# A graph attention kernel: second-layer softmax whose sums come out of the last product

## The chip, the cores and the metric

The kernel runs on one core of one Trainium2 chip. The metric is the device time of one execution in microseconds (us). Before the change it is 2752.51 us, the median of three runs (2750.7, 2752.51 and 2756.27).

The core's engines work in parallel, each through its own instruction stream: TensorE (PE in the profile; PEld is its loading of weights) multiplies matrices into eight PSUM banks, VectorE (DVE) and ScalarE (ACT) compute element by element and empty the banks, GpSimd (POOL) issues some of the transfers and does small work, SyncE (SP) issues the other transfers. An instruction waits until those whose results it needs are done; a stream is worked off in order.

## The reference

32 independent graphs (B = 32) have N = 512 nodes with D = 512 features each. After a layer normalisation and a ReLU come two graph attention layers, the first with 4 heads of 256 features, the second with one head of 512; the input is added at the end.

```python
h = jnp.maximum(_layernorm(x, axis=-1), 0.0)
# gat_layer(h, mask, W, a_src, a_dst, bias):
xl = (x @ W).reshape(B, N, H, F)
asrc = einsum('bnhf,hf->bnh', xl, a_src); adst = einsum('bnhf,hf->bnh', xl, a_dst)
e = leaky_relu(asrc[:, :, None, :] + adst[:, None, :, :], 0.2)
e = where(mask[..., None], e, -1e9)
attn = softmax(e, axis=1)                 # over the sources s
out = einsum('bsdh,bshf->bdhf', attn, xl) # concat (layer 1) or mean (layer 2), + bias
# layer 1, then elu, then layer 2; x + result
```

The mask is the adjacency matrix with the diagonal added. All is fp32.

## The kernel before

**Batches and stages.** A batch is one graph. Node rows are cut into NT = 4 blocks of P = 128 partitions. The main loop (`for i in range(B - 1)`) overlaps batches: while one batch is in its second layer, the next is in its first. A turn of the loop has these products on TensorE: the rest of layer 1's attention product (`gather1`), layer 1's projection of a later batch (`project1`), the second layer's attention product (`gather2`), and the second layer's projection of the next batch (`project2`). The last batch, 31, has plain versions of some of these.

**Products.** Most matrix products are split into 2 x 2 blocks and done in seven block products instead of eight (the Winograd form of Strassen's scheme), numbered 1 to 7. `sevens` (L1170) issues them for `project2` and `gather2`. The result of a product is accumulated in PSUM on top of earlier ones; `ACC` (L1154) says in which bank of its unit: products 1, 6, 7 and 4 follow each other in bank "a", 5 and 3 in "b", 2 has bank "g". A unit u (0 or 1) is a block of 128 output rows within each half. After each product `put` moves what stands in the bank (an eviction): product 1's result is a part of block (0, 0), product 2's is the other part, 6 and 3 belong to block (0, 1), 4 to (1, 0), 5 and 7 to (1, 1) (`BLOCK`, L1152). In `gather2` every one of the 14 evictions of a batch is a VectorE addition of 128x256 from the bank onto the residual tile, which holds the input x and is stored when its block row is complete. The next product into the same bank waits for the eviction. `NEAR` (L1580) is the order of the products: 1, 5, 6, 2, 7, 3, 4, each for both units. `PARTS` (L1213) is the order for batch 29, whose product is interleaved with the last projection. Each block product of `gather2` is two matmuls of 128x128 by 128x256.

The right-hand blocks of `gather2` are the second layer's features, in `xl2` (for the last two batches in memory that is free by then); `project2` leaves them in two halves of 257 columns, and the 257th column of a half is a score of the node. `scores_2` (L1527) reads these columns. `sums2` (L1554) forms the sums and differences of blocks that the products need: t1, t2, t4 in three free slots of the x tiles (`xs`, L604), others in place.

**Softmax.** It runs over sources, which lie on the partitions in the product, so it is done in two passes (`Soft`). `columns` makes the score columns and spreads one of them over all partitions (`spread`: a transposition on VectorE, a small transfer to DRAM, and one back that repeats it 128 times). `first` (L1005), with targets on the partitions, does four blocks d of 128 targets, each over all 512 sources:

```python
act(..., e, o[:, j, :], AF.Prelu, bias=z[:, 1, j, d : d + 1], alpha=SLOPE)    # leaky ReLU of the score sums
dve(..., nc.vector.tensor_tensor_reduce, out=e3, in0=e3, in1=mt[:, :, d, :], ...)  # mask, and -maximum
act(..., e, e, AF.Exp, bias=low[:, 0, d : d + 1], scale=-1.0, accum_out=low[:, 1, d : d + 1])  # sums
```

then a logarithm of the four sums, and spreads (score - maximum - log of the sum) over the partitions. `second` (L1058), with sources on the partitions, forms the scores again (VectorE multiply-adds), adds the mask by accumulating transfers from DRAM (issued by GpSimd), and takes the exponential (ScalarE), which is then the normalised attention matrix p.

**Order of the work.** Nothing is issued as the functions above run: `act`, `dve`, `dma`, `accumulate` and `pe` (L645 to L660) add a job to a `Program` with an estimated cost and the keys that it reads and writes. `Program.order` lays TensorE's jobs down in the order in which they were added, simulates all engines, and searches for an order of the other engines' jobs that lets TensorE wait least. A change of any job thus changes the order of the whole. `Banks.take` gives a bank; with `kept`, only a bank whose columns were last written up to that width, since a matmul is then to add to what another engine put there (a fork: ScalarE copies one bank into another, and a product is added on top).

The profile names the helper line where a job is recorded: L646 ScalarE, L649 VectorE, L652 SP's transfers, L657 the accumulating transfers, L663 matmuls. In the profile's tile names mm is a bank, p the attention matrix, t the residual, l the tile e of the first pass, rr and as the spread rows, z and low small columns, x the x slots.

Of the kernel before, what the change touches and what calls it, by code (L numbers as in the profile page):

```python
# [15 lines left out]
AF = mybir.ActivationFunctionType  # L16
OP = mybir.AluOpType
# [3 lines left out]
P = 128  # L21
EPS = 1e-5
SLOPE = 0.2
BIG = 2.0**100
# [488 lines left out]
def tile_gat(  # L513
# [46 lines left out]
    KQ = KT // 2  # L560
    KH = FT // 2
    W2H = DO // 2 + 1
    assert N == 512 and D == 512 and DO == D and FH == 256 and H == 4

    sbuf = ctx.enter_context(tc.tile_pool(name="sbuf", bufs=1))
# [35 lines left out]
    hs = sbuf.tile([P, 2, KH, N // 2], F32, name="hs")  # L601
    hs4 = sbuf.tile([P, KQ, N // 2], F32, name="hs4")

    xs = slots("x", NT, [P, D])  # L604
    adjs = slots("adj", 2, [P, N], I32)
    xrs = slots("xr", 3, [P, N])
    ls = slots("l", 3, [P, N])
# [5 lines left out]
    rrs = slots("rr", 2, [P, 2, N])  # L613
    das = slots("das", 2, [2 * NT, P], F32, dram)
    drs = slots("drr", 2, [2 * NT, P], F32, dram)
    mds = slots("dm", 3, [P, NT, N], BF16, dram)
    stats = slots("stats", 2, [P, NT, nc.vector.BN_STATS_DIM + nc.vector.BN_AGGR_DIM + 1])
    zs = slots("z", 4, [P, 5, 2, NT])
    lows = slots("low", 3, [P, 4, NT])
    banks = Banks(tiles("mm", 8, [P, 512], F32, psum))  # L620


# [4 lines left out]
                tensor=w1_sb.tensor, offset=w1_sb.offset + NT * (DO + 2) + i * NT * N,  # L627
                ap=[w1_sb.ap[0], [N, NT], [1, N]],
# [7 lines left out]
        ap=[w1_sb.ap[0], [1, NT * N // 2]],  # L636
# [6 lines left out]
    prog = Program()  # L643

    def act(cost, reads, writes, *a, **k):  # L645
        prog.add("ACT", cost, reads, writes, lambda: nc.scalar.activation(*a, **k))  # L646

    def dve(cost, reads, writes, f, *a, **k):
        prog.add("DVE", cost, reads, writes, lambda: f(*a, **k))  # L649
# [302 lines left out]
    class Soft:  # L952
# [52 lines left out]
        def first(self, h, parts=((0, NT),)):  # L1005


            i, j = divmod(h, self.g)
            zk, z, keys = self.z[i]
            ok, o = self.asr[i]  # L1010
            tk, mt = MASKT[self.b]
            wk, low = lows.take()
            zj = z[:, 1, j]
            self.rr[h] = []
            for d0, d1 in parts:
                for d in range(d0, d1):
# [33 lines left out]
                v = bass.AP(tensor=low.tensor, offset=to, ap=[low.ap[0], [1, 2 * n]])  # L1050
                self.rr[h].append((d0, d1, *self.spread(v, [wk + (2, d0)], 2, rrs, drs, n)))
            lows.give(wk)
            if j == self.g - 1:
                ass.give(ok)
            if self.layer == 2:
                mts.give(tk)

        def second(self, h):  # L1058
            i, j = divmod(h, self.g)
# [107 lines left out]

        return put

    def sevens(left, right, rkeys, put, kh, units, width, order, seeds={}):  # L1170


        bank, sixth = {}, len({u for u, _ in order})
        for u, n in order:
            m = units[u][0]
            acc, first = ACC[n], n in (1, 2, 5)
            if first:
                bank[u, acc] = banks.take(width, M if n in seeds else 0)
            bk, bt = bank[u, acc]
            ps = bt[:, :width]  # L1180
            if first and n in seeds:
                first = False
# [28 lines left out]
    FOUR = LAST + tuple((u + 2, n) for u, n in LAST)  # L1211

    PARTS = (  # L1213
        (0, 1), (1, 1), (0, 2), (1, 2), (0, 5), (1, 5), (0, 6), (1, 6), (0, 3), (1, 3), (0, 7), (1, 7),
        (0, 4), (1, 4),
    )

# [284 lines left out]
    def x2_key(b, t, c):  # L1502
        return ("x2", b, t, c) if b >= B - LATE else ("xl2", t, c)
# [50 lines left out]
    def sums2(b, soft, place=None, keys=None):  # L1554

        pk, p = soft.p[0]
        blocks = half_blocks(p, KQ, lambda r, c: p_keys(pk, (2 * c, 2 * c + 1), (r,)))
        left = sums(blocks, KQ, 0.59, KQ, place, keys)
        v = x2(b)
        b11, b12, b21, b22 = (  # L1560
            (
                v[:, 2 * r : 2 * r + 2, c * W2H : c * W2H + M],
                [x2_key(b, 2 * r + i, c) for i in range(2)],
            )
            for r in range(2) for c in range(2)
        )
        t1, t2, t4 = (
            (t.rearrange("p (k f) -> p k f", f=M), [k]) for k, t in (xs.take() for _ in range(3))
        )

        def op(to, a, c):
            dve(0.59, a[1] + c[1], to[1], nc.vector.tensor_sub, to[0], a[0], c[0])

        op(t1, b12, b11)
        op(t2, b22, t1)
        op(b12, b22, b12)
        op(t4, b21, t2)
        return left, {1: b11, 2: b21, 3: b22, 4: t4, 5: t1, 6: t2, 7: b12}

    NEAR = tuple((u, n) for n in (1, 5, 6, 2, 7, 3, 4) for u in range(2))  # L1580

    def gather2(b, soft, blocks, order=NEAR):
        left, right = blocks
        xr = XR.pop(b)
        upper = [2, 2]

        def put(n, u, bk, ps):
            r, c = BLOCK[n - 1]
            d = 2 * r + u[0]
            place, xk, xt = xr[d]  # L1590
            to = xt[:, c * M : (c + 1) * M]
            dve(ADD, [bk, xk + (c,)], [xk + (c,)], nc.vector.tensor_tensor, to, ps, to, op=OP.add)

            upper[u[0]] -= n in (2, 3)
            if n == 4 or r == 0 and upper[u[0]] == 0:
                upper[u[0]] = -1
                dma(0.65, [xk, xk + (0,), xk + (1,)], (), out[b, d * P : (d + 1) * P, :], xt)
                place.give(xk)

        yield from sevens(  # L1600
            left, lambda n, u, k: right[n][0][:, k, :], lambda n: right[n][1], put, KQ,
            [(0,), (1,)], M, order,
        )
        ps_.give(soft.p.pop(0)[0])
        for n in (4, 5, 6):
            xs.give(right[n][1][0])
# [194 lines left out]
```

## Time and profile before

| | |
|---|---|
| runs | 2750.7, 2752.51, 2756.27 us |
| the profiled execution's span | 2756.9 us, 4.4 us above the median |
| TensorE busy | 2732.9 us, 99% of the span |
| VectorE busy | 2595.0 us, 94% |
| ScalarE busy | 2281.9 us, 83% |
| GpSimd busy | 326.5 us, 12% |
| mean granted TensorE clock | 0.999 |

Busy time is the time in which at least one instruction of the engine was running; instructions of one engine overlap a little, so that the mean duration of one is longer than the distance from one to the next. Each fp32 matmul leaves two records. The span runs from the first to the last instruction of the program.

### The profile page before, as it was taken

What the parts mean: (1) busy time and instruction counts of PE and PEld (TensorE: products, weight loads), DVE (VectorE), ACT (ScalarE), POOL (GpSimd) and SP (SyncE); (2) the same over time, 40 slices, a digit from 0 to 9 for tenths busy, and PEclk for the clock granted to TensorE, in tenths of its full rate; (3) what the DMA queues carried; (4) which work ended last, traced back from release to release, by engine and by line L of the source; (5) the groups of instructions that cost most, each with busy time, mean ns of one, the idle gap of its engine ahead of it and who ended that gap; (6) DMA issues with size and microseconds to landing.
All of it is one profiled execution on the core that took longest, in us unless ns stands there. A gap on an engine that the chain in (4) does not pass through costs nothing.

```text
span 2756.9 us, 41901 instructions
## 1 busy us (share of the span) xinstructions
PE 2732.9 (99%) x12490; PEld 2367.0 (86%) x12490; DVE 2595.0 (94%) x6744; ACT 2281.9 (83%) x4871; POOL 326.5 (12%) x356
## 2 busy tenths in 40 slices
PE   7999999999999999999999999999999999999999
PEld 6688888888888888888888888888888888888887
DVE  8999999999999999999999999999999999999996
ACT  5978898888888888988889887888888898888973
POOL 0111110101111011111011110111111111101110
PEclk9999999999999999999999999999999999999999
DMA  8756866667676677666776666766666766777663
GB/s 225 182 162 181 206 177 173 182 182 194 174 193 176 177 184 206 179 168 183 187 207 173 182 176 183 191 188 182 178 182 180 213 173 172 185 183 199 169 169 108
DMA packets 375863, 502.10 MB, mean 182 GB/s; under 512 B 222804, under 2 KB 227668, under 8 KB 375636
## 3 DMA queue, kind: packets, MB, share of 16 engines
q1 hardware_dynamic: 329844, 332.68, 43.3%
q0 software_dynamic: 45792, 166.74, 24.7%
q8 instruction: 100, 1.64, 0.2%
q14 instruction: 127, 1.04, 0.1%
HBM read 316.41 MB, written 51.31 MB: 133 GB/s over the span
## 4 chain that ended last, share of the span: by engine, by line
PE 97%; DMA 1%; ACT 1%; DVE 0%; SPq 0%; issue 0%; ACTq 0%
PE mm L663 97%; DMA x<-adj 0%; DMA w_sb<-dm 0%; ACT l L646 0%; DMA w_sb<-in_L_gnn_W_dram 0%; DMA as<-das 0%; DMA das<-as 0%; SPq L652 0%; DVE h L649 0%; ACT x L646 0%; DVE hs L649 0%; ACT ht L646 0%; DVE w_sb L649 0%; ACT w_sb L646 0%; DVE xl L649 0%
## 5 line engine op out<-in xcount | busy, mean ns | idle before, releaser
L663 PE MATMUL mm<-w_sb,hs 128*128 128x257 f32 (+2 forms) x3032 | 696.4, 380 | 2.2 <-ACT xl L646 1.6
L663 PEld LDWEIGHTS mm<-w_sb,hs 128*128 128x128 f32 x3032 | 575.3, 190 | 87.7 <-ACT xl L646 2.4
L657 POOL DMA_DIRECT2D p<-dm x314 | 274.3, 878 | 2330.5 <-DVE p L649 1312.6
L646 ACT ACTIVATE l<-l,low 128x512 f32<-128x512 f32 x640 | 458.2, 719 | 23.1 <-DVE low L649 20.6
L663 PE MATMUL mm<-w_sb,h 128*128 128x257 f32 x2056 | 467.9, 379 | 0.0
L663 PE MATMUL mm<-p,xl 128*128 128x256 f32 (+1 forms) x1984 | 466.6, 383 | 0.0
L649 DVE SCALAR_TENSOR_TENSOR p<-rr,z 128x512 f32<-128x512 f32 (+1 forms) x636 | 453.8, 739 | 0.0
L646 ACT ACTIVATE l<-as,z 128x512 f32<-128x512 f32 x640 | 436.7, 714 | 17.4 <-DMA as<-das 16.7
L663 PEld LDWEIGHTS mm<-w_sb,h 128*128 128x128 f32 x2056 | 389.2, 189 | 58.1 <-issue 0.5
L646 ACT ACTIVATE p<-p,z 128x512 f32<-128x512 f32 (+1 forms) x636 | 422.0, 718 | 11.3 <-DVE p L649 8.4
L649 DVE CUSTOM_DVE_ANT_1 l<-l,mt 128x512 f32<-128x512 f32 x640 | 424.8, 681 | 4.4 <-ACT l L646 2.3
L663 PEld LDWEIGHTS mm<-p,xl 128*128 128x128 f32 x1984 | 377.3, 190 | 58.8 <-issue 6.9
L663 PE MATMUL mm<-w_sb,ht 128*128 128x258 f32 x1802 | 419.5, 382 | 2.9 <-ACT ht L646 2.9
L663 PEld LDWEIGHTS mm<-w_sb,ht 128*128 128x128 f32 x1802 | 340.7, 190 | 55.7 <-ACT ht L646 3.3
L646 ACT ACTIVATE h<-mm,b_sb 128x256 f32<-128x256 f32 (+1 forms) x504 | 226.2, 475 | 184.5 <-PE mm L663 183.8
L646 ACT ACTIVATE xl<-mm 128x258 f32<-128x258 f32 (+2 forms) x686 | 258.3, 380 | 84.0 <-PE mm L663 80.6
L649 DVE TENSOR_TENSOR xl<-xl,mm 128x258 f32<-128x258 f32 (+1 forms) x526 | 215.4, 416 | 51.6 <-PE mm L663 47.4
L663 PE MATMUL mm<-t,hs 128*128 128x256 f32 x992 | 226.1, 380 | 0.0
L663 PEld LDWEIGHTS mm<-t,hs 128*128 128x128 f32 x992 | 189.0, 191 | 26.1 <-DVE t L649 0.3
L649 DVE TENSOR_TENSOR t<-mm,t 128x256 f32<-128x256 f32 (+1 forms) x424 | 171.7, 417 | 15.8 <-PE mm L663 13.3
L646 ACT ACTIVATE xr<-h 128x512 f32<-128x512 f32 x256 | 157.6, 624 | 34.5 <-DVE h L649 32.9
L663 PE MATMUL mm<-xl,p 128*128 128x256 f32 (+1 forms) x752 | 179.3, 387 | 0.0
(132 smaller groups left out, 3451.2 us busy)
## 6 DMA issues: line engine op xcount, KB each, us to landing
p<-dm POOLq DMA_DIRECT2D x314, 512.0 KB, 4.9
rr<-drr SPq DMA_DIRECT2D x159, 512.0 KB
x<-in_x_dram SPq DMA_DIRECT2D x129, 256.0 KB
adj<-in_adj_dram SPq DMA_DIRECT2D x128, 256.0 KB
as<-das SPq DMA_DIRECT2D x64, 512.0 KB
t<-in_x_dram SPq DMA_DIRECT2D x124, 256.0 KB
out_dram<-t SPq DMA_DIRECT2D x124, 256.0 KB
dm<-m SPq DMA_DIRECT2D x64, 256.0 KB
```

The costliest lines, as they stand in the source:

```text
L646: prog.add("ACT", cost, reads, writes, lambda: nc.scalar.activation(*a, **k))
L649: prog.add("DVE", cost, reads, writes, lambda: f(*a, **k))
L657: lambda: nc.gpsimd.dma_start(to, at, accum_op=OP.add), size,
L663: f(*a, **k)
```

## The change

In the second layer of all batches but the last, the softmax is no longer normalised before the product.

- `first` calls the new `bounds` where `summed` says so (layer 2, not the last batch). It takes the masked maximum directly over the spread scores (the leaky ReLU is monotonic, so it can be applied to the four maxima afterwards, by two small VectorE operations). The Prelu, the Exp with its sums and the logarithm on ScalarE fall away. What is spread is (score - maximum).
- The sums come out of the product: the score column behind the blocks B11 and B21, and one behind t1, are set to 1.0 by GpSimd (two memsets in `sums2`), and the products 1, 2 and 5 take 257 columns instead of 256. The x slots are made two columns wider for this.
- Product 2 must stand on top of product 1 for the sums of the upper rows, so ScalarE copies the bank of product 1 into product 2's bank (a fork), and product 2 adds to it. Product 1 is then not evicted by itself.
- `put` takes the reciprocal of the 257th column after products 2 and 5 (VectorE, one column each), and each of the 12 evictions that are left multiplies by it and adds.
- The orders change so that 2 comes ahead of 6 in `NEAR`, and 5 ahead of 2 in `PARTS`.

```diff
     def first(...):
             for d0, d1 in parts:
+                if self.summed():
+                    self.bounds(j, d0, d1, wk, low, ok, o, keys, zk, zj, h)
+                    continue
...
+        def bounds(self, j, d0, d1, wk, low, ok, o, keys, zk, zj, h):
+            tk, mt = MASKT[self.b]
+            n = d1 - d0
+            for d in range(d0, d1):
+                lk, e = ls.take()
+                dve(
+                    0.62, [ok, tk + (0,), tk + (1,)], [lk, wk + (0, d)], nc.vector.tensor_tensor_reduce,
+                    out=e.rearrange("p (t r) -> p t r", r=P),
+                    in0=o[:, j].rearrange("p (t r) -> p t r", r=P), in1=mt[:, :, d, :], scale=-1.0,
+                    scalar=BIG, op0=OP.add, op1=OP.min, accum_out=low[:, 0, d : d + 1],
+                )
+                ls.give(lk)
+            dve(TINY, ..., nc.vector.tensor_sub, low[:, 1, d0:d1], zj[:, d0:d1], low[:, 0, d0:d1])
+            dve(TINY, ..., nc.vector.scalar_tensor_tensor,
+                low[:, 0, d0:d1], low[:, 1, d0:d1], SLOPE, low[:, 1, d0:d1], op0=OP.mult, op1=OP.max)
+            dve(TINY, ..., nc.vector.tensor_tensor, ..., op=OP.subtract)
+            self.rr[h].append((d0, d1, *self.spread(v, [wk + (2, d0)], 2, rrs, drs, n)))
...
     def sevens(..., forks=False):
             if first:
-                bank[u, acc] = banks.take(width, M if n in seeds else 0)
+                bank[u, acc] = banks.take(width, M if n in seeds else width if forks and n == 2 else 0)
...
+            if forks and n == 2:
+                first = False
+                ak, at = bank[u, "a"]
+                act(0.29, [ak], [bk], ps, at[:, :width], AF.Copy)
+            if forks and n not in (1, 2, 5):
+                ps = bt[:, :M]
...
     PARTS = (
-        (0, 1), (1, 1), (0, 2), (1, 2), (0, 5), (1, 5), (0, 6), (1, 6), (0, 3), (1, 3), (0, 7), (1, 7),
+        (0, 1), (1, 1), (0, 5), (1, 5), (0, 2), (1, 2), (0, 6), (1, 6), (0, 3), (1, 3), (0, 7), (1, 7),
...
     def sums2(...):
+        k1 = t1[1][0]
+        w1 = wide[k1[1]].rearrange("p (k f) -> p k f", f=W2H)
+        t1 = w1[:, :, :M], [k1]
+        first = [x2_key(b, t, 0) for t in range(NT)]
+        prog.add("POOL", 0.3, S2[b].z[0][2], first, lambda: nc.gpsimd.memset(v[:, :, M : M + 1], 1.0))
+        prog.add("POOL", 0.3, (), [k1], lambda: nc.gpsimd.memset(w1[:, :, M:], 1.0))
         op(t1, b12, b11)
...
-    NEAR = tuple((u, n) for n in (1, 5, 6, 2, 7, 3, 4) for u in range(2))
+    NEAR = tuple((u, n) for n in (1, 5, 2, 6, 7, 3, 4) for u in range(2))
...
         def put(n, u, bk, ps):
+            if n == 1:
+                return
...
-            dve(ADD, [bk, xk + (c,)], [xk + (c,)], nc.vector.tensor_tensor, to, ps, to, op=OP.add)
+            if n in (2, 5):
+                dve(TINY, [bk], [ik + (d,)], nc.vector.reciprocal, inv[:, d : d + 1], ps[:, M : M + 1])
+            dve(
+                0.39, [bk, ik + (d,), xk + (c,)], [xk + (c,)], nc.vector.scalar_tensor_tensor,
+                to, ps[:, :M], inv[:, d : d + 1], to, op0=OP.mult, op1=OP.add,
+            )
```

More of the change, by code (lines that the diff above doesn't have):

```diff
@@ L562, in tile_gat @@
     W2H = DO // 2 + 1
+    M2 = DO // 2
     assert N == 512 and D == 512 and DO == D and FH == 256 and H == 4
@@ L602, in tile_gat @@
     hs4 = sbuf.tile([P, KQ, N // 2], F32, name="hs4")
-    xs = slots("x", NT, [P, D])
+    wide = tiles("x", NT, [P, 2 * (M2 + 1)])
+    xs = Slots("x", [t[:, :D] for t in wide])
     adjs = slots("adj", 2, [P, N], I32)
@@ L619, in tile_gat @@
     lows = slots("low", 3, [P, 4, NT])
+    invs = slots("inv", 2, [P, NT])
     banks = Banks(tiles("mm", 8, [P, 512], F32, psum))
@@ L1056, in first, with summed @@
                 mts.give(tk)
+        def summed(self):
+            return self.layer == 2 and self.b < B - 1
+        def bounds(self, j, d0, d1, wk, low, ok, o, keys, zk, zj, h):
[10 more added lines that the diff above has]
+                ls.give(lk)
+            lo = [wk + (0, d) for d in range(d0, d1)]
+            dve(
+                TINY, lo + keys, [wk + (1, d0)], nc.vector.tensor_sub,
+                low[:, 1, d0:d1], zj[:, d0:d1], low[:, 0, d0:d1],
+            )
+            dve(
+                TINY, [wk + (1, d0)], lo, nc.vector.scalar_tensor_tensor,
+                low[:, 0, d0:d1], low[:, 1, d0:d1], SLOPE, low[:, 1, d0:d1], op0=OP.mult, op1=OP.max,
+            )
+            to = low.offset + 2 * (NT + d0)
+            dve(
+                TINY, lo + keys + [zk + (2,)], [wk + (2, d0)], nc.vector.tensor_tensor,
+                bass.AP(tensor=low.tensor, offset=to, ap=[low.ap[0], [n, 2], [1, n]]),
+                bass.AP(tensor=zj.tensor, offset=zj.offset + d0, ap=[zj.ap[0], [4 * NT, 2], [1, n]]),
+                low[:, 0:1, d0:d1].to_broadcast([P, 2, n]), op=OP.subtract,
+            )
+            v = bass.AP(tensor=low.tensor, offset=to, ap=[low.ap[0], [1, 2 * n]])
+            self.rr[h].append((d0, d1, *self.spread(v, [wk + (2, d0)], 2, rrs, drs, n)))
         def second(self, h):
@@ L1168, in signed, with sevens @@
         return put
-    def sevens(left, right, rkeys, put, kh, units, width, order, seeds={}):
+    def sevens(left, right, rkeys, put, kh, units, width, order, seeds={}, forks=False):
         bank, sixth = {}, len({u for u, _ in order})
@@ L1177, in sevens @@
             if first:
-                bank[u, acc] = banks.take(width, M if n in seeds else 0)
+                bank[u, acc] = banks.take(width, M if n in seeds else width if forks and n == 2 else 0)
+                if not bank[u, acc]:
+                    raise RuntimeError("no bank")
             bk, bt = bank[u, acc]
             ps = bt[:, :width]
+            if forks and n == 2:
[4 more added lines that the diff above has]
+                ps = bt[:, :M]
             if first and n in seeds:
@@ L1572, in op @@
             dve(0.59, a[1] + c[1], to[1], nc.vector.tensor_sub, to[0], a[0], c[0])
+        k1 = t1[1][0]
+        w1 = wide[k1[1]].rearrange("p (k f) -> p k f", f=W2H)
+        t1 = w1[:, :, :M], [k1]
+        first = [x2_key(b, t, 0) for t in range(NT)]
+        prog.add(
+            "POOL", 0.3, S2[b].z[0][2], first, lambda: nc.gpsimd.memset(v[:, :, M : M + 1], 1.0)
+        )
+        prog.add("POOL", 0.3, (), [k1], lambda: nc.gpsimd.memset(w1[:, :, M:], 1.0))
         op(t1, b12, b11)
@@ L1577, in sums2 @@
         op(t4, b21, t2)
+        t1 = w1, [k1]
+        b11, b21 = (
+            (v[:, 2 * r : 2 * r + 2, :W2H], [x2_key(b, 2 * r + i, 0) for i in range(2)]) for r in range(2)
+        )
         return left, {1: b11, 2: b21, 3: b22, 4: t4, 5: t1, 6: t2, 7: b12}
-    NEAR = tuple((u, n) for n in (1, 5, 6, 2, 7, 3, 4) for u in range(2))
+    NEAR = tuple((u, n) for n in (1, 5, 2, 6, 7, 3, 4) for u in range(2))
     def gather2(b, soft, blocks, order=NEAR):
@@ L1585, in gather2 @@
         upper = [2, 2]
+        ik, inv = invs.take()
         def put(n, u, bk, ps):
+            if n == 1:
+                return
             r, c = BLOCK[n - 1]
@@ L1591, in put @@
             to = xt[:, c * M : (c + 1) * M]
-            dve(ADD, [bk, xk + (c,)], [xk + (c,)], nc.vector.tensor_tensor, to, ps, to, op=OP.add)
+            if n in (2, 5):
+                dve(TINY, [bk], [ik + (d,)], nc.vector.reciprocal, inv[:, d : d + 1], ps[:, M : M + 1])
+            dve(
+                0.39, [bk, ik + (d,), xk + (c,)], [xk + (c,)], nc.vector.scalar_tensor_tensor,
+                to, ps[:, :M], inv[:, d : d + 1], to, op0=OP.mult, op1=OP.add,
+            )
             upper[u[0]] -= n in (2, 3)
@@ L1601, in gather2 @@
             left, lambda n, u, k: right[n][0][:, k, :], lambda n: right[n][1], put, KQ,
-            [(0,), (1,)], M, order,
+            [(0,), (1,)], W2H, order, forks=True,
         )
+        invs.give(ik)
         ps_.give(soft.p.pop(0)[0])
```

## The prediction

> **What bounds the kernel now.** I read the page first: busy shares and the chain that ended last.
>
> ```profile
> span 2756.9 us, 41901 instructions
> PE 2732.9 (99%) x12490; PEld 2367.0 (86%) x12490; DVE 2595.0 (94%) x6744; ACT 2281.9 (83%) x4871; POOL 326.5 (12%) x356
> ...
> PE 97%; DMA 1%; ACT 1%; DVE 0%; SPq 0%; issue 0%; ACTq 0%
> ```
>
> TensorE is busy for 99% of the span and carries 97% of the chain. A share of 99% says little when matmuls overlap, so next come the busy times in stretches (each engine's busy us, records in brackets, then granted clock):
>
> ```profile
> 655.00:663.00 8.00, 5.83 (x26) 4.46 (x25) 7.62 (x19) 7.85 (x19) 0.86 (x1) 1.00 1.04 289
> 663.00:2665.00 2002.00, 2002.00 (x9233) 1749.36 (x9234) 1910.35 (x4903) 1700.05 (x3635) 239.53 (x259) 1.00 0.69 183
> 2665.00:2692.00 27.00, 24.53 (x104) 20.18 (x103) 23.72 (x51) 17.75 (x36) 3.48 (x4) 0.94 0.53 139
> ```
>
> Between 663 and 2665 us TensorE is never idle: 9233 records in 2002 us are 216.8 ns each at clock 1.00. That must be held against the rate at which it can stream, which the order of time shows for products 258, 257 and 256 columns wide:
>
> ```profile
> 2374.47 5.38 PE L663 MATMUL mm<-w_sb,hs 128*128 128x258 f32 x24
> 2379.69 3.64 PE L663 MATMUL mm<-w_sb,ht 128*128 128x258 f32 x16
> 2383.17 1.89 PE L663 MATMUL mm<-xl,p 128*128 128x256 f32 x8
> ...
> 2692.39 5.38 PE L663 MATMUL mm<-w_sb,h 128*128 128x257 f32 x24
> ...
> 2716.74 1.89 PE L663 MATMUL mm<-xl,p 128*128 128x256 f32 x8
> ...
> 2728.92 3.61 PE L663 MATMUL mm<-x,h 128*128 128x256 f32 x16
> ...
> 2737.55 1.89 PE L663 MATMUL mm<-x,p 128*128 128x256 f32 x8
> ```
>
> From start to start: 258 columns take (2379.69-2374.47)/24 = 217.5 ns a record, 257 take (2716.74-2692.39)/112 = 217.4 (112 records stand between these rows), 256 take (2737.55-2728.92)/40 = 215.75. Each matmul leaves two records. A batch has 55 matmuls of 258 columns, 56 of 257 and 84 of 256 (28 of these in the second layer's last product), so free streaming would be 216.7 ns a record. The kernel runs 0.1 ns above it: 9233 x 0.11 ns, about 1 us, is all that is lost in 2002 us. One batch is 390 x 216.8 ns = 84.6 us. In it VectorE idles (2002.00-1910.35)/23.7 = 3.9 us and ScalarE 12.8 us.
>
> So the order was planned such that VectorE and ScalarE hide fully, and relief for ScalarE can buy only the few idle pieces outside that window.
>
> **The change part by part.** The rows that price it (mean ns of one behind the busy time):
>
> ```profile
> L646 ACT ACTIVATE l<-l,low 128x512 f32<-128x512 f32 x640 | 458.2, 719 | 23.1 <-DVE low L649 20.6
> L646 ACT ACTIVATE l<-as,z 128x512 f32<-128x512 f32 x640 | 436.7, 714 | 17.4 <-DMA as<-das 16.7
> L646 ACT ACTIVATION_READ_ACCUMULATOR l<-l,low 128x1 f32 x640 | 125.3, 196 | 0.0
> L646 ACT ACTIVATE low<-low 128x4 f32<-128x4 f32 x159 | 32.1, 202 | 0.5
> L646 ACT ACTIVATE mm<-mm 128x256 f32<-128x256 f32 x120 | 44.4, 374 | 10.7 <-PE mm L663 8.7 <-DVE z L649 0.5 <-DVE t L649 0.5
> L649 DVE TENSOR_TENSOR t<-mm,t 128x256 f32<-128x256 f32 x420 | 168.9, 414 | 7.5 <-PE mm L663 5.1
> L649 DVE SCALAR_TENSOR_TENSOR p<-rr,z 128x256 f32<-128x256 f32 x8 | 3.5, 476 | 0.0
> L649 DVE SCALAR_TENSOR_TENSOR stats<-stats 128x4 f32<-128x4 f32 x32 | 5.1, 159 | 1.9 <-POOL stats L892 1.9
> L649 DVE COPY z<-mm 128x2 f32<-128x2 f32 x16 | 2.3, 153 | 0.7 <-ACT w_sb L646 0.7
> L892 POOL TENSOR_TENSOR stats<-stats,half 128x4 f32<-128x4 f32 x32 | 52.6, 1643 | 44.2 <-DVE stats L649 41.1 <-ACT l L646 3.2
> ```
>
> *ScalarE, 31 batches of 32.* Out go 4 Prelu (714), 4 Exp (719), 4 accumulator reads (196) and the Ln (202): 6.72 us a batch. In come two fork copies at 374: 0.75. Net -5.97 us a batch, 185 us in all. None of it lies on the chain in the 2002 us window, so I put its gain there at 0.
>
> *TensorE.* Products 1, 2 and 5 widen from 256 to 257 columns: 3 products x 2 units x 2 matmuls x 2 records x 31 = 744 records. By the difference of the rows, 217.4-215.75 = 1.65 ns, that is 1.2 us; in proportion to the columns (215.75/256 = 0.84 ns) 0.6 us. I take 1.2, the direct difference. This is on the path and nothing hides it.
>
> *VectorE.* The masked maximum stays as it is, reading the spread scores instead of the Prelu's output. Out go two additions at the banks (product 1): -2 x 414. In come four reciprocals of one bank column (nearest row the 128x2 copy out of a bank, 153): +0.61 us; one more tiny operation in the first pass, +0.16; and 12 additions become multiply-adds with a scalar from a tile. No row has that out of a bank; the same form from SBUF takes 476, the plain addition 414, so 0 to 62 ns each, and I take 62: +0.74. Sum +0.69 us a batch against 3.9 us of idle. It is hidden on average; without that cover it would be 31 x 0.69 = 21 us. [...]
>
> *The order of the products.* This matters more than the sums. Product 2 moves ahead of 6, so between product 6 and product 7 of a unit, which accumulate in the same bank, there is one other product where there were three. VectorE must evict 6 within that one. The trace has the same distance at the end of the first layer's projection (products 7 and 4):
>
> ```profile
> 2380.76 0.42 DVE L649 TENSOR_TENSOR xl<-xl,mm 128x258 f32<-128x258 f32 x1 [0.21 <-PE mm L663]
> 2381.63 0.42 DVE L649 TENSOR_TENSOR xl<-xl,mm 128x258 f32<-128x258 f32 x1 [0.45 <-PE mm L663]
> 2382.21 0.69 DVE L649 TENSOR_TENSOR hs<-p 128x512 f32<-128x512 f32 x1 [0.15 <-ACT p L646]
> ```
>
> Product 7 began at 2379.69, ended 4 records later at 2380.56; its eviction ran 2380.76 to 2381.18 and TensorE went on at 2381.43 without a gap. With 476 ns, 0.863-0.20-0.476 = 0.19 us are left. VectorE had waited for it there (0.21, 0.45 idle). All losses of the window, this place's included, are 1 us, so for the two new places of a batch I take +1.0 us over the kernel. Product 2 itself needs the fork copy; three products (2.6 us) stand before it, and a ScalarE operation in progress (0.72) plus the copy (0.37) fit.
>
> *GpSimd.* Two memsets a batch, bounded by 0 and the 1643 ns row. They stand in its queue among the mask additions that the second Exp waits for, so all of those shift by as much. The ones column waits for the scores to be read, the second for a free x tile; the subtraction t1 waits for both:
>
> ```profile
> 2335.89 0.22 DVE L649 TENSOR_SCALAR z<-xl,c 128x4 f32<-128x4 f32 x1
> ...
> 2357.29 0.69 DVE L649 TENSOR_TENSOR x<-xl 128x512 f32<-128x512 f32 x1
> ...
> 2384.90 3.61 PE L663 MATMUL mm<-x,hs 128*128 128x256 f32 x16
> ```
>
> 21.4 us lie between the scores and t1, 27.6 between t1 and its product. I take 0; without that cover, up to 31 x 2 x 1.64 = 102 us. The spread's two transfers a pass stay; they leave SP earlier, the second pass on VectorE can begin earlier, and nothing in the window waits for it.
>
> *The tail.* After project2 of the last batch, two of these products and the last softmax run together:
>
> ```profile
> 2717.00:2739.00 22.00, 22.00 (x103) 19.06 (x102) 19.95 (x59) 10.20 (x22) 0.00 (x0) 1.00 0.40 133
> ```
>
> VectorE has 2.05 us free there and gets 2 x 0.69 more: 0 to 1.4 us late, I take 0.7.
>
> Sum: 1.2 + 1.0 + 0.7 = +2.9 us. The profiled execution would go from 2756.9 to 2759.8; it lies 4.4 us above the median of the runs, 2752.51, on which I put the sum: 2755.4.
>
> **The rivals.**
>
> *Slower: VectorE comes late at the banks of product 6.* If it is in the middle of a 128x512 operation (0.69 us) when product 6 ends, the eviction starts on average 0.34 us late, 0.15 beyond the 0.19 left: 62 x 0.15 = 9.3 us in place of the 1.0, 2763.7; at worst 62 x 0.50 = 31 us, 2785. It decides from 5.5-1.9 = 3.6 us on, 0.06 us a place. For it: VectorE is 95% busy and gets heavier. Against it: the projection's end.
>
> *Slower: isolated stalls.* The whole order is planned anew. At the end of the trace one stall shows its price:
>
> ```profile
> 2674.06 1.47 PE L663 MATMUL mm<-w_sb,xl 128*128 128x256 f32 x4 [1.92 <-ACT w_sb L646]
> 2675.32 1.91 PE L663 MATMUL mm<-p,xl 128*128 128x256 f32 x4
> 2677.03 1.75 PE L663 MATMUL mm<-t,hs 128*128 128x256 f32 x4
> 2678.62 1.03 PE L663 MATMUL mm<-w_sb,xl 128*128 128x256 f32 x4
> ```
>
> After 1.92 us idle, eight records took 3.30 us instead of 1.73: 1.92 + 1.57 = 3.5 us. One more such stall decides; two give 2762.4. [...]
>
> *Faster: the idle pieces close.* ScalarE's l operations stand in the chain before the gap at 660.8. Idle there 2.17 us, at the end 2.47, half clock 1.57, and 2.85 before the stream starts:
>
> ```profile
> 48.92 3.63 PE L663 MATMUL mm<-w_sb,ht 128*128 128x258 f32 x10 [2.85 <-ACT ht L646]
> ```
>
> All gone, with 1.2 for the columns: 2752.5 + 1.2 - 9.1 = 2744.6. The last piece lies before any second layer, and the median run already stands 4.4 below this one.
>
> **How the numbers follow.** I count 0.2%, 5.5 us, as what a measurement of this kernel can tell from no change: its three runs lie that far apart. Forecast 2755.4, chance 0.50, own range 2750 to 2758; late at the banks 0.27; isolated stalls 0.15; faster 0.08. Range 2747 to 2768: it leaves out most of the faster case and the dear end of the banks. Faster 0.08, same 0.50, slower 0.42.
>
> **What would show it.** TensorE without idle from the first batch to the last, two records 216.8 ns apart on average; ScalarE's busy time near 2097 us; VectorE's near 2616; multiply-adds out of banks near 476 ns. I am wrong if product 7 of the last product starts late batch after batch, if GpSimd's memsets hold t1, or if the tail's softmax slips by several us.

## The result and the profile after

The changed kernel takes 2767.65 us (median of four runs, 2762.82 to 2769.78). The kernel before, run beside it, takes 2753.47 us. The ratio is 1.0047, 95% interval 1.0035 to 1.0059: slower by 0.47%, some 13 us by the ratio.

The page of the changed kernel, the same lines as shown of the kernel before:

```profile
span 2761.1 us, 41790 instructions
PE 2738.6 (99%) x12490; PEld 2358.3 (85%) x12490; DVE 2612.2 (95%) x6837; ACT 2147.8 (78%) x4530; POOL 337.6 (12%) x418
...
PE 93%; DVE 3%; DMA 3%; ACT 1%; issue 1%; SPq 0%; DVEq 0%; ACTq 0%
```

ScalarE's share fell from 83% to 78% and VectorE's rose from 94% to 95%. TensorE still has 99%, but the chain now leaves it: 93% in place of 97%, the rest goes through VectorE and transfers. This profiled execution is the fastest of the four runs, and part of the loss is hidden by a quicker start: the unbroken stream of matmuls begins at 45.9 us in place of 48.9. So the better measure is how much work TensorE finishes in one stretch of the loop. The view by stretches from 60 to 2650 us, of the kernel before and then of the changed one (busy us of TensorE first, with its matmul records in brackets):

```profile
60.00:2650.00 2590.00, 2587.83 (x11869) 2248.79 (x11869) 2468.03 (x6361) 2201.45 (x4698) 315.86 (x340) 1.00 0.69 183
```

```profile
60.00:2650.00 2590.00, 2587.10 (x11830) 2235.65 (x11829) 2473.68 (x6422) 2063.03 (x4347) 325.81 (x398) 1.00 0.69 183
```

The busy times differ by 0.7 us, yet the changed kernel got through 39 records less. At 2590/11869 = 218.2 ns each, that is 8.5 us. Busy time hides it: in the profile a record of 128x256 lasts 378 ns in the mean, while the next starts 216 ns behind it (kernel before, `mm<-xl,p`), so that a start up to 162 ns late leaves no idle time. The number of records in a stretch is the honest figure, and I use it for all kernels below.

Part of the loss is where the prediction had looked. The order of time, changed kernel, second layer's last product of one batch, TensorE and then VectorE:

```profile
2385.18 1.90 PE L666 MATMUL mm<-xl,p 128*128 128x257 f32 x8
2386.92 1.90 PE L666 MATMUL mm<-x,hs 128*128 128x257 f32 x8
2388.66 1.90 PE L666 MATMUL mm<-xl,p 128*128 128x257 f32 x8
2390.39 1.89 PE L666 MATMUL mm<-x,hs 128*128 128x256 f32 x8
2392.41 2.00 PE L666 MATMUL mm<-xl,p 128*128 128x256 f32 x8
2394.24 1.89 PE L666 MATMUL mm<-xl,hs 128*128 128x256 f32 x8
2395.97 1.89 PE L666 MATMUL mm<-x,p 128*128 128x256 f32 x8
2397.70 0.60 PE L666 MATMUL mm<-w_sb,h 128*128 128x257 f32 x2
```

```profile
2390.67 0.67 DVE L652 SCALAR_TENSOR_TENSOR h<-xr,h 128x512 f32<-128x512 f32 x1
2391.26 0.69 DVE L652 CUSTOM_DVE_ANT_1 l<-l,mt 128x512 f32<-128x512 f32 x1
2391.87 0.08 DVE L652 DVE_READ_ACCUMULATOR2_ANT low<- 128x1 f32 x1
2391.87 0.93 DVE L652 SCALAR_TENSOR_TENSOR t<-mm,inv,t 128x256 f32<-128x256 f32 x2
```

These rows are the products 1, 5, 2, 6, 7, 3, 4, both units each. Product 6 of unit 0 ends at 2390.39 + 4 x 0.216 = 2391.25. VectorE has just begun a masked maximum (2391.26) and evicts only at 2391.87. Product 7 starts at 2392.41, though eight records after 2390.39 TensorE would have been free at 2392.12. Then 7 itself takes 2.00 us where eight such records take 1.89. From the start of product 1 to the first matmul behind the last one, these 28 matmuls took 12.52 us here. In the kernel before they start at 2383.17 in the prediction's rows, and the first matmul behind them is

```profile
2395.26 5.38 PE L663 MATMUL mm<-w_sb,h 128*128 128x257 f32 x24
```

so they took 12.09 us, and they did so in each of the 29 batches in which this product stands alone on TensorE. Over these batches the mean went from 12.09 to 12.27 us: 29 x 0.18 = 5.3 us, of which the wider columns are 0.02 a batch (a batch without a late product takes 12.114).

### The profile page after: what moved, and what is told of

Read it like the earlier page. It is cut to its first block, busy times and chain, and to the rows that moved or that the text cites. A ratio compares the mean times of both kernels' runs of the same rounds, so it can differ in the third digit from the quotient of the medians.

```text
span 2761.1 us, 41790 instructions
## 1 busy us (share of the span) xinstructions
PE 2738.6 (99%) x12490; PEld 2358.3 (85%) x12490; DVE 2612.2 (95%) x6837; ACT 2147.8 (78%) x4530; POOL 337.6 (12%) x418
## 4 chain that ended last, share of the span: by engine, by line
PE 93%; DVE 3%; DMA 3%; ACT 1%; issue 1%; SPq 0%; DVEq 0%; ACTq 0%
PE mm L666 93%; DMA mt<-m 1%; DMA x<-adj 1%; DVE l L652 0%; DVE h L652 0%; DVE t L652 0%; DMA p<-dm 0%; DVE xr L652 0%; DVE hs L652 0%; DMA adj<-in_x_dram 0%; ACT l L649 0%; DVE p L652 0%; DVE w_sb L652 0%; DMA rr<-drr 0%; DMA p<-in_L_gnn_att_dst_dram 0%
## 5 line engine op out<-in xcount | busy, mean ns | idle before, releaser
L649 ACT ACTIVATE p<-p,z 128x512 f32<-128x512 f32 (+1 forms) x636 | 427.7, 713 | 23.5 <-DMA p<-dm 12.8
L649 ACT ACTIVATE l<-l,low 128x512 f32<-128x512 f32 x516 | 367.9, 715 | 17.7 <-DVE low L652 16.2
L649 ACT ACTIVATE l<-as,z 128x512 f32<-128x512 f32 x516 | 352.1, 713 | 21.2 <-DMA as<-das 20.7
L652 DVE CUSTOM_DVE_ANT_1 l<-l,mt 128x512 f32<-128x512 f32 x516 | 344.8, 684 | 10.7 <-ACT l L649 8.1
L666 PE MATMUL mm<-xl,p 128*128 128x257 f32 (+1 forms) x752 | 187.8, 391 | 0.7 <-DVE t L652 0.4
L652 DVE SCALAR_TENSOR_TENSOR h<-xr,h 128x512 f32<-128x512 f32 x256 | 173.5, 686 | 3.0 <-ACT xr L649 2.6
```

## The experiments

Three theories were tested. *Bank*: VectorE comes late at the bank of product 6, because one product stands between 6 and 7 in place of three. *Load*: VectorE's reciprocals and multiply-adds are too much, wherever they stand. *Plan*: the order of all queues is searched anew whenever a job changes, and the order found for the changed kernel stalls more.

**The changed kernel again**, without an edit.

> The changed kernel once more, on the chip of the three runs below, for a second profile of it. Theory bank (VectorE comes late at the bank of product 6, because one product stands between 6 and 7 where there were three): product 7 of the second layer's last product starts late by 0.1 to 0.6 us in most batches again, some 4 to 5 us in all, and the kernel takes about 2767 us. Theory plan (any change gives a new order of all work, and the new order has scattered stalls): the stalls outside the last product stand at the same places as in the first profile of it and cost more than those at product 7.

2771.57 us, ratio 1.0058 (1.0043 to 1.0073). The last product took 12.27 us in the mean again, and the same products 7 were late (in 26 of 29 batches), most of them by the same time within some nanoseconds: this loss belongs to the order. Stalls elsewhere stood at the same places and were larger: in the first half of the loop TensorE's waits at 262, 317 and 437 us had been at 260, 315 and 433. The stretch from 60 to 2650 us:

```profile
60.00:2650.00 2590.00, 2580.85 (x11793) 2227.84 (x11792) 2467.07 (x6406) 2057.07 (x4330) 324.34 (x397) 1.00 0.70 182
```

That is 76 records less than the kernel before, or 16.6 us, where the first profile of the same kernel had lost 8.5. The chain that ended last, in order of time, at the wait at 262 us (start us, length us):

```profile
251.70 9.42 DMA mt<-m
...
261.25 0.69 DVE l L652
...
264.30 0.43 DVE xl L652
264.73 0.04 issue
264.78 1.42 PE mm L666 x5
```

and what VectorE and TensorE did there, in order of time:

```profile
261.25 0.69 DVE L652 CUSTOM_DVE_ANT_1 l<-l,mt 128x512 f32<-128x512 f32 x1 [3.39 <-DMA mt<-m]
...
264.30 0.42 DVE L652 TENSOR_TENSOR xl<-xl,mm 128x258 f32<-128x258 f32 x1
```

```profile
264.78 2.07 PE L666 MATMUL mm<-w_sb,ht 128*128 128x258 f32 x8 [2.42 <-DVE xl L652]
```

The transposed mask landed 9.4 us after it was issued. VectorE waited 3.39 us for it, and behind the waiting maximum, in the same queue, stood the eviction that TensorE needed: a late transfer became 2.42 us of idle TensorE through a queue that works in order. In the first profile of the same kernel the same transfer took 8.26 us, and TensorE waited 1.25 us.

**The order of the products alone**, on the kernel before:

```diff
-    NEAR = tuple((u, n) for n in (1, 5, 6, 2, 7, 3, 4) for u in range(2))
+    NEAR = tuple((u, n) for n in (1, 5, 2, 6, 7, 3, 4) for u in range(2))
```

> The kernel before with one line changed: the products of the second layer's last product in the order 1, 5, 2, 6, 7, 3, 4. Nothing else of the change, evictions are plain additions of 0.41 us. Theory bank: product 7 starts late in many batches, by less than in the changed kernel since the eviction is 0.06 us shorter: 2 to 3 us in all, time 2755 to 2757. Theory load (VectorE's reciprocals and multiply-adds are what is too much): no late product 7, 2752 to 2755 as before. Theory plan: stalls anywhere in the loop, 2753 to 2765.

2783.68 us, ratio 1.0103 (1.0086 to 1.012), worse than the whole change, and more than any of the theories had asked for. Late products 7 are there with plain additions too, but fewer (in 9 of 29 batches against 26). Most of the 29 us are other stalls: theory plan is the nearest. This kernel has no fork, no memset and no multiply-add, so none of these is needed for such stalls.

**The first pass alone**, on the kernel before: `bounds` and its call, and nothing else of the change.

> The kernel before with the first pass of the change alone: maxima without Prelu, Exp, sums and logarithm. The division is left out, so the attention isn't normalised. ScalarE loses 6.7 us a batch, VectorE gains one tiny operation, the order of the products is the old one. Theories bank and load: TensorE has no stall at the last product, 2749 to 2754, no gain beyond the few idle pieces. Theory plan: scattered stalls as in the changed kernel, 2755 to 2765.

2790.28 us, ratio 1.0127 (1.0109 to 1.0146): less work in every batch, and 36 us more. TensorE's waits (waiter, what ended the wait, us in total, times, longest):

```profile
PE mm L663 <- ACT x L646: 11.0, 3, 10.2
PE mm L663 <- ACT p L646: 8.4, 1, 8.4
PE mm L663 <- DVE hs L649: 6.9, 3, 5.1
PE mm L663 <- ACT later L646: 4.2, 1, 4.2
```

The 10.2 us in the first line are the start, which all kernels have. The next three lines are five waits, the longest 8.4 us; in the kernel before the longest wait behind the start is 2.9 us. The mean granted clock was 0.996 here and 0.999 in the kernel before, and the eight records behind one wait of 5.07 us took 3.47 us, where eight such records take 1.89: part of the loss is a slower TensorE behind the long waits.

**The division alone**: the changed kernel with the first pass of the kernel before.

```diff
-            return self.layer == 2 and self.b < B - 1
+            return False
```

> The changed kernel with the first pass of the kernel before: p is normalised as before, and the sums from the product (all 1) divide once more. It has the new order, the fork copies, the reciprocals and the multiply-adds, without the relief of ScalarE. Theory bank: product 7 late as in the changed kernel, 2762 to 2768. Theory load: dearer than the changed kernel, 2768 to 2775, as ScalarE's work isn't taken off. Theory plan: stalls at other places than in the changed kernel, 2755 to 2770.

2765.09 us, ratio 1.0036 (1.0023 to 1.0049). The last product took 12.30 us in the mean. Giving back ScalarE's relief costs nothing that shows, though this kernel has an order of its own too; theory load, which asked for 2768 or more, is not supported.

**The first pass in the old order.** This takes the work and the order apart, which the two runs before could not. The jobs and their estimates stay as in the kernel before, so the search ends with the same order; only the instructions of Prelu, Exp, accumulator reads and Ln are not issued:

```diff
+                    bare = self.layer == 2 and self.b < B - 1
+                    def work(cost, reads, writes, *a, **k):
+                        if bare:
+                            prog.add("ACT", cost, reads, writes, lambda: None)
+                        else:
+                            act(cost, reads, writes, *a, **k)
...
-                    act(
+                    work(
                         0.62, [ok, *keys], [lk], e, o[:, j, :], AF.Prelu,
...
-                        out=e3, in0=e3, in1=mt[:, :, d, :], scale=-1.0, scalar=BIG,
+                        out=e3, in0=o3 if bare else e3, in1=mt[:, :, d, :], scale=-1.0, scalar=BIG,
```

> The kernel before in exactly its order, with the work of Prelu, Exp, accumulator reads and Ln of the second layer's first pass not issued in 31 batches (the maximum is taken over the spread scores; the normalisation and the leaky ReLU of the maxima are left out). ScalarE loses 6.7 us a batch, no queue changes its order otherwise. Theory plan: what made the first pass alone 36 us slower was its new order; here the time is 2748 to 2754. Theory of the first pass (an earlier or lighter first pass itself brings transfers into each other's way): 2765 or more.

2753.06 us, ratio 0.9998 (0.9988 to 1.0008). The page and the stretch:

```profile
PE 2730.7 (99%) x12490; PEld 2367.0 (86%) x12490; DVE 2594.5 (94%) x6744; ACT 2138.8 (78%) x4468; POOL 328.7 (12%) x356
```

```profile
60.00:2650.00 2590.00, 2589.54 (x11880) 2252.06 (x11879) 2470.75 (x6367) 2065.86 (x4315) 318.16 (x340) 1.00 0.70 183
```

ScalarE is relieved by 143 us and TensorE finishes 11 records more (2.4 us), which the median of the runs does not resolve. In the traces VectorE, GpSimd and TensorE work through the same sequence of operations as in the kernel before. So the relief is worth nothing measurable, and the 36 us of the first pass alone came with its new order; besides the order it differs only by tiny VectorE operations on the maxima (160 ns each, one more in a batch), which no run measures by themselves.

**The division without its work, in the changed kernel's order**: the reciprocals issue nothing and the evictions are plain additions.

```diff
-                dve(TINY, [bk], [ik + (d,)], nc.vector.reciprocal, inv[:, d : d + 1], ps[:, M : M + 1])
+                prog.add("DVE", TINY, [bk], [ik + (d,)], lambda: None)
             dve(
-                0.39, [bk, ik + (d,), xk + (c,)], [xk + (c,)], nc.vector.scalar_tensor_tensor,
-                to, ps[:, :M], inv[:, d : d + 1], to, op0=OP.mult, op1=OP.add,
+                0.39, [bk, ik + (d,), xk + (c,)], [xk + (c,)], nc.vector.tensor_tensor,
+                to, ps[:, :M], to, op=OP.add,
             )
```

> The changed kernel in exactly its order: the same estimates lead to the same queues, but the reciprocals issue nothing and the evictions are plain additions, so the attention is not normalised. VectorE loses 1.4 us of work a batch, all else is the same, instruction by instruction. Theory load (VectorE's new work is what is too much): 2753 to 2757, late products 7 below 1 us in all, the other stalls back at about 8 us. Theory bank: late products 7 fall from 4.5 us to about 2 (the eviction ends 0.06 us earlier and waits for no reciprocal), the other stalls hardly change, 2762 to 2767. Theory plan (the order is what is worse): both kinds of stalls stay within 3 us of the changed kernel, 2764 to 2770.

2765.97 us, ratio 1.0039 (1.0024 to 1.0054). Products 7 are late in only 4 of 29 batches, and the last product takes 12.15 us in the mean in place of 12.27. In the order of time VectorE is now at the bank in time, and TensorE goes from 6 to 7 without a gap:

```profile
2394.74 0.42 DVE L652 TENSOR_TENSOR t<-mm,t 128x256 f32<-128x256 f32 x1
2395.60 0.42 DVE L652 TENSOR_TENSOR t<-mm,t 128x256 f32<-128x256 f32 x1 [0.44 <-PE mm L666]
```

But the stalls elsewhere stay: 11820 records in the same stretch, against 11830 and, in its second profile, 11793 of the changed kernel. In this order the division's work on VectorE explains most of the lateness at product 7, 29 x 0.12 = 3.5 us, and none of the rest. One of the stalls elsewhere is the wait at 262 us again, at the same matmul:

```profile
263.33 3.26 PE L666 MATMUL mm<-w_sb,ht 128*128 128x258 f32 x8 [2.47 <-DVE xl L652]
```

**Staggered units**: the changed kernel with at least two products between any product and the next in its bank; between 6 and 7 there are three in unit 0 and two in unit 1.

```diff
-    NEAR = tuple((u, n) for n in (1, 5, 2, 6, 7, 3, 4) for u in range(2))
+    NEAR = (
+        (0, 1), (1, 1), (0, 5), (0, 2), (0, 6), (1, 2), (1, 6), (1, 5), (0, 7), (1, 7), (0, 3), (1, 3),
+        (0, 4), (1, 4),
+    )
```

> The changed kernel with the two units' products staggered so that at least two products stand between any product and the next one in its bank (three between 6 and 7 where the change has one), and two ahead of the product on the fork. Theory bank: no late product 7, less than 1 us of stalls inside the last product in all batches together; by itself 4 to 5 us less than the changed kernel, 2763 to 2766. Theory load: stalls inside the last product stay. Theory plan: the rest of the time moves by 5 to 30 us either way with the new order, whatever becomes of product 7.

2769.86 us, ratio 1.0048 (1.0031 to 1.0065). No product 7 is late in any batch, and the last product takes 12.12 us in the mean: theory bank is right about the place. The time did not fall, because the stalls outside took it back (11812 records in the stretch; the first line is the start):

```profile
PE mm L666 <- ACT x L649: 11.4, 2, 11.1
PE mm L666 <- ACT mm L649: 3.3, 1, 3.3
PE mm L666 <- DVE hs L652: 3.1, 4, 1.4
PE mm L666 <- ACT xl L649: 2.9, 2, 1.9
```

**No division, order searched anew**: plain additions and no reciprocals as jobs, so that the search sees less work.

```diff
-            if n in (2, 5):
-                dve(TINY, [bk], [ik + (d,)], nc.vector.reciprocal, inv[:, d : d + 1], ps[:, M : M + 1])
-            dve(
-                0.39, [bk, ik + (d,), xk + (c,)], [xk + (c,)], nc.vector.scalar_tensor_tensor,
-                to, ps[:, :M], inv[:, d : d + 1], to, op0=OP.mult, op1=OP.add,
-            )
+            dve(ADD, [bk, xk + (c,)], [xk + (c,)], nc.vector.tensor_tensor, to, ps[:, :M], to, op=OP.add)
```

> The changed kernel with plain additions at the banks: no reciprocals, no multiplication, so the attention is not normalised; columns of ones, fork copies and the order of the products stay. VectorE loses 1.4 us a batch. Theory load: no stalls at product 7, and 2752 to 2757. Theory bank: product 7 still late, as the distance of one product stays, but by less (2 to 3 us in all instead of 4 to 5). Theory plan: the rest moves by 5 to 30 us either way.

2820.57 us, ratio 1.0241 (1.0224 to 1.0258), the slowest of all, with less work than the changed kernel; no theory had asked for that. Products 7 are late in 20 of 29 batches and the last product takes 12.30 us in the mean, as long as with the division: a lighter eviction doesn't cure the place in every order. 34.5 us are six waits of one kind:

```profile
PE mm L666 <- DVE hs L652: 34.5, 6, 11.1
```

Against the run in the changed kernel's order with the same evictions, 55 us are the order. Some of that is the clock: its mean was 0.992 here and 0.999 there, which over 2819 us is some 20 us at most, an estimate (0.007 x 2819).

**How far the order moves a kernel whose work is unchanged.** Two runs search the kernel before anew, one with another seed (`Random(2)`), one with one estimate changed:

```diff
-    COPY, ADD, TINY = 0.28, 0.34, 0.1
+    COPY, ADD, TINY = 0.28, 0.34, 0.101
```

> The kernel before with another seed for the random part of the planner's search (Random(2) for Random(1)): the same instructions in another order. Theory plan: the time is no property of the work; it moves by 5 to 30 us, to 2757 to 2785, through isolated stalls of 1 to 5 us behind late transfers, and the last product has no late product 7. Theory bank or load alone: 2750 to 2757 as before.

> The kernel before with one number of the planner changed: the cost estimate of tiny VectorE operations is 0.101 us instead of 0.100. The same instructions, another order. Theory plan (the order the search ends with decides over some 10 us, whatever the work): 2757 to 2770, by isolated stalls. If the order of the kernel before is nothing special: 2751 to 2757.

The seed: 2759.7 us, ratio 1.0016 (1.0005 to 1.0027). The estimate: 2760.47 us, ratio 1.0028 (1.0018 to 1.0038). The last product took 12.09 us in every batch in both. Not one instruction was added or taken away. The times are those of theory plan, but its isolated stalls don't show: the stretches of the two, in the same order,

```profile
60.00:2650.00 2590.00, 2588.71 (x11869) 2248.20 (x11869) 2469.14 (x6364) 2204.60 (x4698) 315.55 (x340) 1.00 0.70 183
```

```profile
60.00:2650.00 2590.00, 2587.38 (x11866) 2248.33 (x11865) 2467.16 (x6359) 2199.64 (x4692) 318.21 (x340) 1.00 0.70 183
```

hold as many records as that of the kernel before (11869). Both profiled executions are the fastest of their runs (2756.1 and 2757.27 us), so what makes the medians longer by 0.16 and 0.28% was not seen.

**Other orders of the changed kernel**: another seed, and the staggered products with seed 4.

> The changed kernel with the other seed. Theory plan: anywhere from 2757 to 2790, isolated stalls at other places than in the changed kernel. Theory bank: whatever the order, product 7 of the last product starts late in most batches by 0.1 to 0.6 us, 4 to 5 us in all.

> The staggered products with another seed of the search (4), picked among several as the one in which the kernel's planner leaves TensorE the fewest waits. Theory bank with plan: no late product 7, and isolated stalls of 8 to 15 us instead of 21: 2757 to 2765, below the changed kernel and not below the kernel before. If it is below 2753, the change can pay with a good order.

2780.15 us, ratio 1.0088 (1.0073 to 1.0103), with products 7 late in 28 of 29 batches; and 2777.73 us, ratio 1.0087 (1.0072 to 1.0102), with none late, above the 2757 to 2765 expected. In this one case the search's own count of waits was no guide to a good order. No order of the changed kernel that was run comes near the kernel before.

## Why the prediction was right or wrong

The forecast, no measurable change at 2755.4 us, did not come: the kernel is slower by 0.47%. The range (2747 to 2768) holds the median by a hair, which is luck: the second measurement, 2771.57 us, lies outside it. "Slower" had been given 0.42. The two rivals on that side came about together, which the prediction had not reckoned with: each had a chance and a price of its own, and their sum, 2763.7 + 7.0 = 2770.7, had none.

- *TensorE is the bound, ScalarE's relief is worth 0.* Right, and shown in the old order: 0.9998. ScalarE's busy time fell by 134 us, not 185: durations on one engine overlap, so a sum of durations overstates what busy time loses. In the kernel before an Exp of 0.73 us starts at 2380.13, its accumulator read of 0.21 us at 2380.74, and the next operation at 2380.84.
- *Wider columns, +1.2 us.* Taken too large: 12.114 against 12.090 us for a last product without a late start, 31 x 0.024 = 0.7 us. The estimate in proportion to the columns, 0.6, was the better one.
- *VectorE +0.69 us a batch, hidden on average.* The prices were right: a multiply-add out of a bank measures 476 ns, a reciprocal 160; VectorE's busy time is 2612 us, forecast 2616. So the row with a scalar from a tile was the right one to go by. The plain additions last 414 ns in the prediction's row, the multiply-adds 476 ns in the first row here.

```profile
L652 DVE SCALAR_TENSOR_TENSOR t<-mm,inv,t 128x256 f32<-128x256 f32 x360 | 165.2, 476 | 2.3 <-PE mm L666 1.0
...
L652 DVE RECIPROCAL inv<-mm 128x1 f32<-128x1 f32 x124 | 19.3, 160 | 4.4 <-PE mm L666 3.4
...
L1629 POOL MEMSET xl<- 128x4 f32 x30 | 13.9, 462 | 0.0
...
L1631 POOL MEMSET x<- 128x2 f32 x31 | 3.5, 113 | 407.8 <-ACT ht L649 361.2 <-DVE h L652 17.6 <-PE mm L666 14.8
```

- *The order of the products, +1.0 us.* The place and the mechanism were right, the size was not: "for the two new places of a batch I take +1.0 us over the kernel" measured 29 x (12.273 - 12.114) = 4.6 us. The projection's end, from which it was taken, is a place where the queue leaves VectorE idle before the eviction (0.21 and 0.45 us); at the new place it is in the middle of 0.69 us operations. The staggered order removes it whole, and the lighter eviction in the same order removes 3.5 us of it.
- *GpSimd's memsets, 0.* Not tested by itself. They take 0.46 and 0.11 us each, and neither stands in the chains read here. But the second waits 408 us in all for its x tile, in the queue that also issues the mask additions, and ScalarE's waits for these grew from 2.9 us before to 12.8 and 20.6 us in the two profiles of the changed kernel. The order of the products alone and the first pass alone, which have no memsets, show 9.5 and 33.8 us, so the memsets aren't needed for such waits; that they add to them is not excluded.
- *The tail, +0.7 us.* From the last projection to the last product it took 2743.01 - 2695.26 = 47.75 us, before 2739.28 - 2692.39 = 46.89: +0.9 us. The changed kernel's two rows, then the one of the kernel before that the prediction doesn't show:

```profile
2695.26 5.38 PE L666 MATMUL mm<-w_sb,h 128*128 128x257 f32 x24
...
2743.01 13.91 PE L666 MATMUL mm<-xl,p 128*128 128x512 f32 x32
```

```profile
2739.28 13.91 PE L663 MATMUL mm<-xl,p 128*128 128x512 f32 x32
```

- *Isolated stalls, only a rival at 0.15.* This is the step that failed. I took the new order of the whole to be as free of stalls as the one in the profile. The runs show that this can't be taken for granted: the same work with two products exchanged costs 1.03%, a first pass with less work 1.27%. Two other orders of the kernel before cost only 0.16 and 0.28%, so that its own order is an exception is not shown. In the changed kernel some 8 to 11 us are put down to stalls, by subtraction: the 14 to 17 us between its medians and those of the kernel before in the two measurements, less 4.6 for product 7 and 1.6 for columns and tail. The records of the stretch, less 5.3 us for the last product, give 3 us in the first profile and 11 in the second: the same order costs more in one execution than in another. The half clock, which had made a stall dear in the prediction (3.5 us for 1.92), was no part of it: the granted clock was 1.00 in the loop in both profiles of the changed kernel, with waits of up to 2.42 us. In other runs the clock did fall, and there a stall cost more than its length: around a wait of 2.47 us in the run without the division's work it was 0.79 over 8 us, and the eight records behind that wait took 3.05 us in place of 1.91.

What stays open is why the orders found for the changed kernel are worse than those found for the kernel before. Three orders of the latter lie at 1 to 1.0028 and four of the former at 1.0047 to 1.0088 (the staggered ones among them). These are few orders, kernels with a part of the change and an order of their own lie at 1.0036 to 1.0241, and no run shows a cause. It isn't the division's load on VectorE, since the lighter evictions left these stalls as they were. The fork copies and the memsets were not taken out in the changed kernel's order. That a better order of the changed kernel exists was not excluded, and none was found.

## What to carry to other kernels

Where a planner lays out the queues, an edit has two effects, its work and its new order, and the second can be many times the first. Measure them apart by keeping the jobs and estimates and taking out only the instructions: that showed nothing measurable for a part that had looked like 36 us. When two products share a bank, count the products between them, and ask what the engine that empties the bank is doing at that moment, not how busy it is on average.

## What the runs showed of the hardware that was not expected

A matmul that had to wait made the next record late as well. In the last products of the changed kernel, wherever the first record of a product 7 came late, the second came 320 ns behind it in place of 216, so that a start that was 12 ns late (228 ns behind the record ahead) cost 116 ns. The rows above show it as 2.00 us for eight records in place of 1.89. Where only the second record came late, the loss was 22 to 111 ns. Of the 26 late batches 20 lost less than 0.18 us. And busy time doesn't show such losses at all: 39 missing records stand against 0.7 us of busy time.

In these runs the length of a wait alone didn't decide whether the clock fell. Behind the 2.42 us at one matmul of the changed kernel it stayed at 1.00; behind 2.47 us at the same matmul, in the run without the division's work, it fell, to a mean of 0.79 over 8 us; in the kernel before it fell behind 1.92 us, to 0.50 from 2675.08 to 2678.49 us. The stretches of the first two, in this order (the granted clock is the third number from the end):

```profile
262.00:270.00 8.00, 5.58 (x26) 4.44 (x25) 8.00 (x22) 7.97 (x20) 0.00 (x0) 1.00 0.01 3
```

```profile
262.00:270.00 8.00, 6.67 (x23) 5.53 (x24) 6.92 (x19) 6.76 (x17) 0.00 (x0) 0.79 0.01 2
```

The eight records behind the wait took 1.91 us from start to start in the first case (264.78 to 266.69) and 3.05 in the second (263.33 to 266.38).
